# Three in-place ScalarE copies ahead of each scatter product in a two-layer GCN and attention kernel

## The chip, the cores and the metric

The kernel runs on one core of a Trainium2 chip. The metric is device time in microseconds (us) of one execution, as a median over runs.

## What is computed

The reference takes 12,500 nodes with 256 features each and 200,000 edges, sorted by destination. All is float32. Cut to what matters:

```python
h = maximum(layernorm(x), 0)
h = h @ W_pre + b_pre
h = relu(gcn(h, W1, b1));  h = relu(gcn(h, W2, b2))     # each: segment_sum(h[src] * norm, dst)
x = x + (h @ W_post + b_post)
h = maximum(layernorm(x), 0)
xt = (h @ weight).reshape(n, 4, 64)
alpha = softmax(leaky_relu(alpha_l(xt[src]) + alpha_r(xt[dst])), axis=1)
x = x + broadcast(einsum('nh,nhd->nd', alpha[:n], xt[dst[:n]]))
```

The two `gcn` layers gather a row of 256 features for every edge and add it to the edge's destination. That is nearly all of the work.

## The kernel before

**Tiles and chunks.** The edges are cut into chunks of 14 tiles of 128 edges (`J = 14`, 1,792 edges); there are `NCH` = 112 chunks, the last of 9 tiles. Each `gcn` layer is one pass, one call of `convolve`, over all chunks. The destination nodes are cut into `NT` = 98 windows of 128 nodes.

**One tile.** GpSimd (POOL) issues an indirect DMA that gathers 128 rows of the layer's table into a slice of the buffer `fgot` (L1374). TensorE (PE) multiplies it by a one-hot matrix that says which destination within the chunk's window each edge has, and accumulates in PSUM (`facc`, L1382). In float32 that product is two weight loads and two matmuls. The one-hot matrices of a whole chunk, 128 x 14 x 128, are made by a single VectorE (DVE) instruction (`hot_of`, L1241), one chunk ahead, at the third tile of the chunk before; there are three such buffers, `fhot`.

```python
            nc.tensor.matmul(acc, hots[c][:, j, :], got[:, :width], start=(j == 0),
                             stop=(j == nj[c] - 1 and not some))
```

**The first chunks of pass 1.** For the chunks 0 to 3 (`raw`, four buffers) the rows were gathered during the preparation, straight from the input; POOL's gathers in the loop begin with the fifth chunk. In pass 2 `raw` is empty. In pass 1 there are five buffers of a chunk's gathers, in pass 2 four, so POOL can run chunks ahead of PE.

**End of a chunk.** `close` has ScalarE (ACT) copy the sums from PSUM (`fsums`, L1276), and puts two steps into a list of due steps: PE turns the sums 8 tiles later (`fturn`, L1206), DVE adds them 13 tiles later into the window's buffer (`buf`, L1293). When a window is complete, its own steps are listed, counted in tiles from that addition. In pass 1 (`finish1`) they are: 6 tiles later a product on PE (`fpo`, L1417 and L1418); 10 tiles later a Relu on ACT (`fo`, L1422) and its DMA to the second layer's table. In pass 2 (`finish2`): 6 PE `fpz` (L1472); 8 DVE `fy` and ACT `fz` (L1479, L1482); 12 PE `fpo` (L1488); 14 DVE `fx`, `st`, `mv` and ACT `sc`, a square root (L1493 to L1501); 16 DVE, then ACT `h` (L1509); 20 PE `fpt` (L1514); 22 ACT `ht` (L1518); 26 PE `fpx` (L1527); 28 ACT `fxa` (L1535) and two DMAs, issued from ACT's queue (L1536, L1538). Near the end of a pass (`near`, the last three chunks) these steps come one tile after another.

**Order.** Each engine works through its instructions in the order in which the program wrote them: for every tile the gather, the product, and then the steps that are due. Every fifth chunk or so ACT also moves the window buffer's contents (`buf`, L1315, and in pass 1 `sbuf`, L1317).

**After pass 2** comes an attention stage of short gathers (`fal`, L1662) and DVE work.

Of the kernel before, what the change touches and what calls it, by code (L numbers as in the profile page):

```python
# [11 lines left out]
AF = mybir.ActivationFunctionType  # L12
# [401 lines left out]
def fast_path(  # L414
# [26 lines left out]
    nc = tc.nc  # L441
# [6 lines left out]
    NCH = -(-E // CE)  # L448
# [84 lines left out]
    def new_got():  # L533
        return gp.tile([P, J, D1], F32, name="fgot", bufs=RAW + 1)

    raw = [new_got() for c in range(RAW)]
# [616 lines left out]
    def convolve(ep, table, stride, width, ahead, with_sum, psum, prepare, finish, lacking=False,  # L1153
                 raw=(), rows_p=None):
# [12 lines left out]
        def at(t, step, fills=None, then=None):  # L1167
            d = {"t": t, "n": state["n"], "step": step, "fills": fills, "then": then}
            state["n"] += 1
            due.append(d)  # L1170
            return d
# [11 lines left out]
        def run(now=None):  # L1183

            while due:
                d = min(due, key=lambda d: (d["t"], d["n"]))
                if now is not None and d["t"] > now:
                    return
                do(d)
# [49 lines left out]
        def one_hots(h, to):  # L1239
            n = to.shape[1]  # L1240
            nc.vector.tensor_tensor(h, iota_p[:, None, :].to_broadcast([P, n, P]),  # L1241
                                    to[:, :, None].to_broadcast([P, n, P]), ALU.is_equal)

        def hot_of(c):

            n = nj[c]
            h = ep.tile([P, J, P], F32, name="fhot", bufs=3)
            one_hots(h[:, :n, :], to_0 if lacking and c == 0 else to_t[:, c, :n])
            return h

        def new_rows_of():
            if with_sum:
                return new_got()
            return rows_p.tile([P, J, stride], F32, name="fgot", bufs=ahead)

        def late_sums():

            h = ep.tile([P, J, P], F32, name="fhot", bufs=3)
            one_hots(h, to_t[:, 0, :])
            froms = new_rows_of()  # L1260
            assert stride == TW * P
            for i in range(TW):
                one_hots(froms[:, :, i * P:(i + 1) * P], from_0[:, i, :])
            px = psum.tile([P, KC, P], F32, name="fpt", bufs=1)
            for i in range(TW):
                for j in range(J):
                    nc.tensor.matmul(px[:, i, :], froms[:, j, i * P:(i + 1) * P], h[:, j, :],  # L1267
                                     start=(j == 0), stop=(j == J - 1))
            many = work.tile([P, KC, P], F32, name="fz", bufs=2)
            nc.scalar.activation(many, px, AF.Copy)  # L1270
            return many, [load_rows((NT - TW + i) * P, P) for i in range(TW)]

        def close(c, acc, t):
# [64 lines left out]
            at(t + (1 if c + 1 == NCH else 2 if near else 8), turn)  # L1338
            at(t + (2 if c + 1 == NCH else 3 if near else 13), add)

        tiles = [(c, j) for c in range(NCH) for j in range(nj[c])]
        hots = {0: hot_of(0)}
        raw_lohi, raw_m = {}, {}
# [7 lines left out]
        def raw_ahead(c, j):  # L1351

            if j == 1:
                raw_hots(raw_lohi[c])
                raw_m[c] = rows_p.tile([P, CE], F32, name="fsources", bufs=1)
            elif j in (3, 5, 7, 9):
                raw_block(raw_lohi[c], raw_m[c], fpt(), 2 * (j - 3))()
                if j == 9:
                    raw_stats(c)
            elif j + 1 == J:  # L1360
                raw_sum(c, raw_m[c], fpt())()
                raw_scaled(c)

        assert KC == TW
        for t, (c, j) in enumerate(tiles):
            if j == 0:
                acc = psum.tile([P, width], F32, name="facc", bufs=2 if not with_sum else 3)

            if j == 0:
                gots = (raw + [spare])[c] if raw and c <= len(raw) else new_rows_of()  # L1370
            got = gots[:, j, :]
            some = lacking and c == 0
            if c >= len(raw):
                nc.gpsimd.indirect_dma_start(  # L1374
                    out=got, out_offset=None, in_=table[:(NT - TW) * P, :] if some else table[:],
                    in_offset=bass.IndirectOffsetOnAxis(
                        ap=src_0[:, j:j + 1] if some else src_t[:, c, j:j + 1], axis=0))
            if j == 2 and some:
                late = late_sums()
            if j == (5 if some else 2) and c + 1 < NCH:  # L1380
                hots[c + 1] = hot_of(c + 1)
            nc.tensor.matmul(acc, hots[c][:, j, :], got[:, :width], start=(j == 0),  # L1382
                             stop=(j == nj[c] - 1 and not some))
            if some and j == nj[c] - 1:
                for i in range(TW):
                    nc.tensor.matmul(acc, late[0][:, i, :], late[1][i], start=False,
                                     stop=(i == TW - 1))
            if j == nj[c] - 1:
                close(c, acc, t)
            if c + 1 < len(raw):  # L1390
                raw_ahead(c + 1, j)
            run(t)
# [39 lines left out]
    with tc.tile_pool(name="psum1", bufs=1, space=PSUM) as psum, \  # L1432
            tc.tile_pool(name="edges1", bufs=1) as ep, \
            tc.tile_pool(name="fwork1", bufs=2) as work, \
            tc.tile_pool(name="flate1", bufs=1) as late:
        attn = load_late(late)
        convolve(ep, table1, D1, D + 1, 4, True, psum, lambda w: prepare1(work, w),
                 lambda w, b, s, pre, _: finish1(work, psum, w, b, s, pre), raw=raw,
                 rows_p=late)
# [141 lines left out]
    with tc.tile_pool(name="psum2", bufs=1, space=PSUM) as psum, \  # L1581
            tc.tile_pool(name="fwork2", bufs=2) as work, \
            tc.tile_pool(name="edges2", bufs=1) as ep, \
            tc.tile_pool(name="fgots2", bufs=1) as rows_p:
        ep.tile([P, 320], F32, name="apart")
        for c in range(EARLY):
            turn_hots(ap, c, load_ends(work, c, 1), EARLY)
        none = work.tile([P, LW, H], F32, name="none", bufs=1)
        nc.vector.memset(none, 0.0)
        nc.sync.dma_start(table_e[(NT - LW) * P:, :].rearrange("(w p) h -> p w h", p=P), none)  # L1590

        from_all = work.tile([P, CE], I32, name="to_all", bufs=1)
        nc.sync.dma_start(from_all, src[:CE].partition_broadcast(P))
        for i in range(LW):
            nc.vector.tensor_scalar(hot_l[i], from_all, float((NT - LW + i) * P), lane,
                                    op0=ALU.subtract, op1=ALU.is_equal)
        convolve(ep, table2, D, D, 4, False, psum, lambda w: prepare2(work, w),
                 lambda w, b, s, pre, bias: finish2(work, psum, w, b, pre, bias), True,
                 rows_p=rows_p)

        for c in range(1, AC):
            own_rows(c)
# [150 lines left out]
```

## Time and profile before

| | |
|---|---|
| median of 12 runs | 4151.65 us (4146.73 to 4158.75) |
| the profiled execution: time, span | 4160.72 us, 4158.9 us |
| PE matmul busy | 3091.8 us (74%) |
| DVE busy | 1139.5 us (27%) |
| ACT busy | 491.9 us (12%) |
| POOL busy | 3113.8 us (75%) |
| gathers of the two passes (L1374) | 3,056, from 130.6 to 3993.8 us of the span |
| first gather of pass 2 | 2028.50 us |
| granted TensorE clock, mean | 0.797 |

The span is what lies between the first and the last instruction of the profiled execution; its own time is 1.8 us more. Busy shares are averages over the whole span: an engine at 75% can still be the one that everything waits for, if the rest is time that it needs between its instructions. A line of a group gives the busy time, the mean duration of one instruction in ns, then the idle time just before such instructions and what ended it.

### The profile page before, as it was taken

Reading aid. Unit: us, or ns where it says so; the run is one execution under the profiler, and the core shown is the slowest. Engines: PE = TensorE matmul, PEld = TensorE weight load, DVE = VectorE, ACT = ScalarE, POOL = GpSimd, SP = SyncE. Lnnn points to the kernel's source line nnn. Section 1 sums busy time; section 2 is a strip of 40 time slices with the busy share of each in tenths; the row PEclk is TensorE's granted clock in tenths of the full one; section 3 lists DMA queues with packets and bytes.
Section 4 is the critical chain, followed back from the end, with each engine's and each line's share of the span. In section 5 each row is a group of like instructions: output and inputs, shape, how many; then the busy total and the mean of one; then the engine's idle time right before and its main releaser. Section 6 shows DMA issues by size and latency. Waiting matters only on the chain. (4 is left out here: it accounts for less than half of the span.)

```text
span 4158.9 us, 32267 instructions
## 1 busy us (share of the span) xinstructions
PE 3091.8 (74%) x10600; PEld 1979.1 (48%) x10600; DVE 1139.5 (27%) x2421; ACT 491.9 (12%) x1233; POOL 3113.8 (75%) x3299
## 2 busy tenths in 40 slices
PE   6688887877888777877577777777777777777774
PEld 5564444444444444443365554554555545545562
DVE  8532111111111111111232222222222222222238
ACT  5400000000000000000011111111111111111122
POOL 7677777777777777777777777777777777777766
PEclk8697778778777788788688888788878888887876
DMA  9644444444444444444545555555555455555556
GB/s 278 189 126 121 119 119 120 122 120 119 119 122 119 119 119 122 119 118 118 151 123 134 129 128 126 129 130 128 127 128 132 128 127 128 131 125 125 132 163 202
DMA packets 327419, 554.57 MB, mean 133 GB/s; under 512 B 96301, under 2 KB 224836, under 8 KB 327244
## 3 DMA queue, kind: packets, MB, share of 16 engines
q0 software_dynamic: 153520, 414.16, 38.9%
q1 hardware_dynamic: 127878, 121.99, 9.9%
q10 hardware_dynamic: 45846, 16.27, 1.6%
q8 instruction: 87, 1.43, 0.2%
q14 instruction: 88, 0.72, 0.1%
HBM read 498.89 MB, written 53.21 MB: 133 GB/s over the span
## 5 line engine op out<-in xcount | busy, mean ns | idle before, releaser
L1374 POOL DMA_INDIRECT fgot<-ftable,fsrc_t x3056 | 2901.2, 949 | 951.3 <-issue 887.9
L1382 PE MATMUL facc<-fgot,fhot 128*128 128x257 f32 (+1 forms) x6252 | 2326.7, 493 | 902.5 <-DMA fgot<-ftable,fsrc_t 861.8
L1382 PEld LDWEIGHTS facc<-fgot,fhot 128*128 128x128 f32 x6252 | 1260.9, 231 | 1808.7 <-DMA fgot<-ftable,fsrc_t 1361.5
L1293 DVE TENSOR_TENSOR buf<-buf,fturn 128x256 f32 x224 | 94.5, 422 | 1635.9 <-PE fturn L1206 1302.9
L1241 DVE TENSOR_TENSOR fhot<-iota_p,to_t 128x1792 f32<-128x1792 f32 x224 | 448.9, 2004 | 5.4 <-PE fpt L1267 5.3
L1479 DVE SCALAR_TENSOR_TENSOR fy<-rb,fb2c,fpz 128x128 f32<-128x128 f32 x194 | 58.8, 344 | 747.4 <-PE fpz L1472 746.4
L1276 ACT ACTIVATE fsums<-facc 128x257 f32<-128x257 f32 (+1 forms) x224 | 86.1, 384 | 1152.6 <-PE facc L1382 1146.5
L1493 DVE SCALAR_TENSOR_TENSOR fx<-fpo,fdinv,fxb 128x256 f32<-128x256 f32 x97 | 46.9, 484 | 478.7 <-PE fpo L1488 478.7
L1417 PE MATMUL fpo<-wf,buf 128*128 128x256 f32 x388 | 154.4, 542 | 0.4 <-DVE buf L1293 0.4
L1422 ACT ACTIVATE fo<-fpo,fdinv 128x256 f32<-128x256 f32 x97 | 46.0, 474 | 749.7 <-PE fpo L1418 749.7
L1417 PEld LDWEIGHTS fpo<-wf,buf 128*128 128x128 f32 x388 | 111.9, 289 | 28.3 <-DVE buf L1293 0.7
L1472 PE MATMUL fpz<-buf,fwb 128*128 128x128 f32 x776 | 123.7, 312 | 0.0
L1472 PEld LDWEIGHTS fpz<-buf,fwb 128*128 128x128 f32 x776 | 120.9, 234 | 2.5 <-DVE fy L1479 0.3
L1488 PE MATMUL fpo<-fwo,fz 128*128 128x256 f32 x388 | 118.1, 432 | 0.1
L1206 PE MATMUL fturn<-fident,self 128*128 128x128 f32 x396 | 84.6, 299 | 37.7 <-DMA to_all<-in_src_dram 24.6
L1662 POOL DMA_INDIRECT fal<-table_l,fsrc_t x84 | 81.7, 973 | 25.6 <-issue 22.9
L1206 PE MATMUL fturn<-fident,fsums 128*128 128x128 f32 x448 | 95.5, 299 | 0.5 <-ACT fsums L1276 0.5
L1652 PE MATMUL fends<-rows,hot_t 128*128 128x260 f32 x168 | 67.5, 567 | 33.7 <-ACT fxg L1654 33.2
L1518 ACT ACTIVATE ht<-fpt 128x256 f32<-128x256 f32 x97 | 37.2, 384 | 466.2 <-PE fpt L1514 466.2
L668 POOL DMA_INDIRECT fgot<-in_x_dram,raw_i x56 | 73.6, 1315 | 15.4 <-issue 15.4
L1206 PEld LDWEIGHTS fturn<-fident,fsums 128*128 128x128 f32 x448 | 70.1, 157 | 31.1 <-issue 8.0
L1418 PE MATMUL fpo<-bb,fins 2*128 2x256 f32 x194 | 84.3, 520 | 0.0
(267 smaller groups left out, 1729.9 us busy)
## 6 DMA issues: line engine op xcount, KB each, us to landing
fgot<-ftable,fsrc_t POOLq DMA_INDIRECT x3056
self<-ftable SPq DMA_DIRECT2D x99, 128.0 KB
self<-ftable SPq DMA_DIRECT2D x97, 130.0 KB
ftable<-fo ACTq DMA_DIRECT2D x98, 128.0 KB
kept_x<-fx SPq DMA_DIRECT2D x98, 128.0 KB
fxb<-in_x_dram SPq DMA_DIRECT2D x97, 128.0 KB
fxr<-kept_x SPq DMA_DIRECT2D x13, 896.0 KB
out_dram<-fres SPq DMA_DIRECT2D x13, 896.0 KB
```

What stands on the lines that cost most here:

```text
L668: nc.gpsimd.indirect_dma_start(out=raw[c][:, j, :D], out_offset=None, in_=x[:], in_offset=bass.IndirectOffsetOnAxis(ap=raw_i[:, k:k + 1], ...
L1206: nc.tensor.transpose(v["pt"][:, i * KC + k, :], rows[:, k * P:(k + 1) * P], ident)
L1241: nc.vector.tensor_tensor(h, iota_p[:, None, :].to_broadcast([P, n, P]), to[:, :, None].to_broadcast([P, n, P]), ALU.is_equal)
L1276: nc.scalar.activation(sb, acc, AF.Copy)
L1293: nc.vector.tensor_add(b, b, v["pt"][:, :KC, :])
L1374: nc.gpsimd.indirect_dma_start(out=got, out_offset=None, in_=table[:(NT - TW) * P, :] if some else table[:], in_offset=bass.IndirectOffset ...
L1382: nc.tensor.matmul(acc, hots[c][:, j, :], got[:, :width], start=(j == 0), stop=(j == nj[c] - 1 and not some))
L1417: nc.tensor.matmul(po, buf[:, k, :P], wf[:, k, :], start=(k == 0), stop=False)
L1418: nc.tensor.matmul(po, fs, bb, start=False, stop=True)
L1472: nc.tensor.matmul(pz[:, m, :], wb[:, k, m * P:(m + 1) * P], buf[:, k, :P], start=(k == 0), stop=(k == KC - 1))
L1488: nc.tensor.matmul(po, v["z"][:, m, :], wo[:, m, :], start=(m == 0), stop=(m == KC - 1))
L1662: nc.gpsimd.indirect_dma_start(out=al[:, i, :], out_offset=None, in_=(table_l if c else table_e)[:], in_offset=bass.IndirectOffsetOnAxis(a ...
```

## The change

Ahead of each product with gathered rows, ScalarE copies the tile's one-hot columns (128 x 128, float32) onto themselves, three times. The values stay the same. This is done for every chunk from number `len(raw)` to the last but one: in pass 1 that is from the fifth chunk on, in pass 2, where `raw` is empty, from the first.

```diff
+        def spread(h):
+            for _ in range(3):
+                nc.scalar.activation(h, h, AF.Copy)
+
         tiles = [(c, j) for c in range(NCH) for j in range(nj[c])]
...
             if j == (5 if some else 2) and c + 1 < NCH:
                 hots[c + 1] = hot_of(c + 1)
+            if len(raw) <= c < NCH - 1:
+                spread(hots[c][:, j, :])
             nc.tensor.matmul(acc, hots[c][:, j, :], got[:, :width], start=(j == 0),
                              stop=(j == nj[c] - 1 and not some))
```

That is 107 chunks in pass 1 and 111 in pass 2, with 14 tiles of three copies each: 9,156 instructions on ACT. The instructions of the other engines and their order stay as they were. In the changed program the second and third copy of a tile wait for ACT's own copy before, each product waits for ACT beside its gather, and each making of one-hots by DVE waits for ACT too.

## The prediction

> **What bounds the kernel now.** I read the page's costliest groups first, for the engine whose idle time nobody else explains. The columns are: busy us, mean ns of one | idle us before it, and what ended it.
>
> ```profile
> L1374 POOL DMA_INDIRECT fgot<-ftable,fsrc_t x3056 | 2901.2, 949 | 951.3 <-issue 887.9
> L1382 PE MATMUL facc<-fgot,fhot 128*128 128x257 f32 (+1 forms) x6252 | 2326.7, 493 | 902.5 <-DMA fgot<-ftable,fsrc_t 861.8
> ```
>
> PE's idle time ends with a gather's landing. POOL's idle time ends with "issue", that is, nothing that the profile shows. The two POOL numbers make 3852.5 us for 3056 gathers, and gathers lie from 130.6 to 3993.8 us: POOL issues them with hardly a break, and that is the kernel's length. Next I read the waits, for POOL's waits on others.
>
> ```profile
> POOL fgot L1374 <- issue: 891.9, 2899, 7.9
> POOL fgot L1374 <- PE facc L1382: 39.3, 104, 7.1
> ```
>
> Only 39.3 us stand against PE, and of the 104 nearly all are the usual 0.30 us; the one of 7.1 is at 147 us, in the raw chunks, which the change leaves alone. Then the timeline of a chunk in the middle of pass 2 (start, us, engine), from the 11th tile on, which the later sums use.
>
> ```profile
> 3016.18 0.94 POOL L1374 DMA_INDIRECT fgot<-ftable,fsrc_t  x1 [0.30 <-issue]
> 3016.51 0.70 PE L1382 MATMUL facc<-fgot,fhot 128*128 128x256 f32 x2 [0.22 <-DMA fgot<-ftable,fsrc_t]
> 3017.43 0.95 POOL L1374 DMA_INDIRECT fgot<-ftable,fsrc_t  x1 [0.30 <-issue]
> 3017.59 0.17 ACT L1535 ACTIVATE fxa<-fpx 128x4 f32<-128x4 f32 x1 [2.80 <-PE fpx L1527]
> 3017.79 0.33 ACTq L1536 DMA_DIRECT2D table_l<-fxa  x1
> 3018.16 1.02 ACTq L1538 DMA_DIRECT2D table_e<-fxa  x1
> 3018.56 0.48 DVE L1493 SCALAR_TENSOR_TENSOR fx<-fpo,fdinv,fxb 128x256 f32<-128x256 f32 x1 [3.89 <-PE fpo L1488]
> 3019.75 0.29 ACT L1501 ACTIVATE sc<-mv,feps 128x1 f32<-128x1 f32 x1 [1.99 <-DVE mv L1499]
> ```
>
> POOL's starts are 1.253 us apart, whatever ACT and DVE do meanwhile; 14 of them make a chunk of 17.54 us. So the question is whether ACT and PE together still get through a chunk in 17.54 us. If they do, up to four chunks of buffers hide every delay within a chunk.
>
> **The price of a copy.** No 128 x 128 copy from SBUF to SBUF is in the trace. The nearest rows, by shape on ACT:
>
> ```profile
> L1482 ACT ACTIVATE fz<-fy 128x256 f32<-128x256 f32 x98 | 40.9, 417 | 219.7 <-DVE fy L1479 219.7
> L1315 ACT ACTIVATE buf<-buf 128x640 f32<-128x640 f32 x46 | 33.9, 737 | 99.1 <-DVE buf L1293 89.8 <-DMA ftable<-fo 6.7 <-ACT fxa L1535 1.8
> L1317 ACT ACTIVATE sbuf<-sbuf 1x320 f32<-1x320 f32 x24 | 10.9, 453 | 3.0 <-DVE sbuf L1296 3.0
> ```
>
> From 417 to 737 ns for 384 elements is 0.833 ns each, so 128 elements cost 417 - 107 = 310 ns by the first row and 453 - 160 = 293 by the third. I take 0.30. For the wait of one copy on the copy before, ACT's timeline in the preparation has such a pair, and a run of instructions without it:
>
> ```profile
> 92.61 3.53 ACT L990 ACTIVATE fgot<-fgot,fnb,fsc 128x256 f32<-128x256 f32 x7
> 96.24 0.16 ACT L941 ACTIVATE fdeg<-fdegs 128x21 f32<-128x21 f32 x1
> 96.44 0.22 ACT L942 ACTIVATE froot<-fdeg 128x21 f32<-128x21 f32 x1
> ```
>
> The dependent one starts 0.20 after one of 0.16: a gap of 0.04, in other pairs 0.03. The seven independent ones of 584 ns start 0.49 apart: they overlap by 0.09. A tile's copies then take 3 x 0.30 + 2 x 0.03 - 0.09 = 0.87 us, a chunk's 14 x 0.87 = 12.2 us.
>
> **ACT's chunk in pass 1.** To the 12.2 come fsums 0.38, fo 0.47 - 0.09, its DMA issue 0.35, and buf and sbuf in 23 of 111 chunks, (0.74 + 0.45) x 23 / 111 = 0.25: 13.6. And one new wait: fsums needs the last tile's product, which now needs the last tile's copies; behind fsums in ACT's queue are the next chunk's copies, and for those PE waits. After the copies comes a product of 0.70 us (the row above, at the full clock), hand-overs of 0.05 and 0.04, and the overlap of 0.09 is lost: 0.88. At half clock a product took 1.22 (3022.99 us), so 1.4. Together 14.4 to 15.0, at least 2.5 us under POOL's chunk: hidden.
>
> **ACT's chunk in pass 2.** 12.2, and with one window's steps fsums 0.38, h 0.59 - 0.09, ht 0.38 - 0.09, fz 0.42 - 0.09, fxa and its two DMA issues 1.0 (median second issue 0.44), less 0.05, sc 0.29 and buf 0.74 x 23 / 111: 2.9, together 15.1. Two waits come on top. At fsums 0.88 again. At sc: ACT gets there after the copies of two tiles and fxa, 1.74 + 0.95 = 2.7 us from the end of the 11th tile's copies; mv is ready after 0.05, that tile's product 0.70, and the 2.54 us from its end at 3017.21 to sc at 3019.75, that is 3.3: a wait of 0.6. The sum is 16.6. A chunk in which no window ends costs 12.2 + 0.3 + 0.88 = 13.4. With 98 windows in 112 chunks the mean is 16.2 us, 1.3 under POOL's.
>
> That is at PE's full clock. In half-microsecond slices the granted clock falls to 0.50 at 3005.2 us, after PE idled from 3002.1, and is back at 1.00 at 3012.2, after 5.5 us of work. At half clock throughout the wait at fsums is 1.4, and at sc the product takes 0.52 and fpx and fpo (1.35 us) another 1.35 more, a wait of 2.5: 19.0 with a window, 18.4 in the mean, 0.9 us over POOL's chunk. From 2600 to 3300 us the clock was 0.82, which is 36% of the time at 0.50; by that share I take 16.2 + 0.36 x 2.2 = 17.0 us, 0.5 under. So pass 2 is hidden too, but narrowly.
>
> The Trainium skill, "TensorE: Matmul & The Clock Gate", section "HAM oscillation", warns of idle gaps over about 3.4 us, after which the array falls back to half clock. The new gaps (fsums and one tile's copies, some 1.3 us) stay under that and by the rule would keep the clock up, so that the sum would be 16.2 rather than 17.0. The same page calls ACT's queue strict FIFO, which speaks against the change, since each of the two waits holds up the copies behind it; the sum above has both.
>
> **What else moves.** Gathers, products and steps keep their order on POOL, PE, DVE and SP. DVE's making of one-hots now waits for copies two chunks old: nothing. ACT's DMA issues stand behind up to 14 tiles' copies, but a tile's step follows that tile's copies, and 12.2 us of 17.54 leaves ACT in time. At the start of pass 2, 12 tiles wait behind the late sums at 2087 us; before, PE took them in 5.35 us, now 12 x 0.87 = 10.4; POOL next needs that buffer at 2105. At the ends there is no slack for free. Pass 2 began when the last rows of the table had landed, 0.98 us after a gather instead of 0.30, so a late ACT in chunk 110 passes through: 0 to 0.9 us. In pass 2's last chunk but one the steps come a tile apart, and each tile could take 0.87 + 0.88 instead of 1.25: 7 us late over 14 tiles, of which PE's waits in the last chunk (2.48 and 1.40) give 3.9 back: 0 to 3.1. I take 2 us of these 0 to 4. None of it can fall below nothing, as the chain only gets a new member.
>
> The profiled execution has 4160.72 us for a span of 4158.9, and is 9.1 us (0.2%) above the median of 4151.65; I add differences to the median: 4151.65 + 2 = 4153.7.
>
> **Rivals.** (1) ACT becomes the bound of pass 2. Its waits for PE outgrow the margin, the buffers fill after some chunks, and POOL starts to wait on PE. It decides from a mean chunk of 17.54 us on, that is from 12 ns more per copy at the mixed clock (31 at the full one). For it: ACT's queue in order, PE's half clock. Against it: a late PE works without breaks, and in 2087 to 2110 us, where it was behind, it took 24 matmuls in 5.35 us, full clock. Price at half clock throughout: 0.86 x 111 = 95 us, 4247; halfway 4200. (2) PE gains. With fewer long idle times its clock stays up, and the chain after the last gather, where matmuls took 2.05, 1.91, 1.37, 1.01 and 0.99 us, would take half of that: 3.7 us less, 4148, still within 0.2%. More would need POOL's 1.253 us to shrink, and nothing in the rows moves it. (3) The copies cost nothing because they are not there: no, the changed program holds 9,156 of them, each with its waits.
>
> **How the numbers follow.** 0.2%, or 8.3 us, is about what a measurement of this kernel can tell from no change. Hidden, with 0 to 4 us at the ends and rival (2) within the bound: 0.60. Rival (1): 0.34, from a few us to 4247 and, if copies are dearer, beyond. Faster by more than 8.3 us: 0.06, for something that I don't see. The likeliest case gives 4153.7 and by itself holds 4146 to 4160. The range goes up to rival (1)'s price, 4247, and down to the lowest run, 4146.
>
> **What would show it.** Right: POOL's starts stay 1.253 us apart in both passes, with waits on PE still near 40 us; ACT busy near 491.9 + 9156 x 0.30 = 3240 us; PE's waits move in part from gathers to copies; copies of 0.29 to 0.31 us, 0.33 apart. Wrong: POOL waiting on PE in hundreds of us in pass 2, a chunk of more than 17.54 us there, or copies over 0.32 us.

## The result, and the profile after

| | before | after |
|---|---|---|
| median | 4151.81 us (28 runs, 4146.73 to 4158.91) | 4194.53 us (7 runs, 4187.79 to 4194.99) |
| the profiled execution: time, span | 4160.72, 4158.9 us | 4193.94, 4192.1 us |
| granted TensorE clock, mean | 0.797 | 0.839 |

The changed kernel takes 1.0098 times as long, 95% interval 1.0088 to 1.0107: 42.7 us more. Ten of the twelve runs told further down were made on four chips on which the kernel before itself took 4,920 to 4,938 us in place of 4,152, so that they are given as ratios to it. The costliest groups of the page after, in the columns of before:

```profile
L1378 POOL DMA_INDIRECT fgot<-ftable,fsrc_t x3056 | 2892.6, 947 | 946.7 <-issue 899.1
L1388 PE MATMUL facc<-fgot,fhot 128*128 128x257 f32 (+1 forms) x6252 | 2302.6, 486 | 1035.1 <-ACT fhot L1343 774.6
L1343 ACT ACTIVATE fhot<-fhot 128x128 f32<-128x128 f32 x9156 | 2562.7, 304 | 281.5 <-ACT fo L1428 38.7
```

POOL's gathers cost what they did, and it still sits idle between them only for "issue". What ended PE's waits has changed from gathers to copies. A copy takes 304 ns. In the view of waits (us in total, times, longest) PE's waits for copies come first, and POOL has one long wait that was 12.9 us before:

```profile
PE facc L1388 <- ACT fhot L1343: 774.6, 1041, 2.8
POOL fal L1668 <- DMA table_l<-fxl: 53.9, 1, 53.9
POOL fgot L1378 <- PE facc L1388: 27.3, 72, 5.7
```

POOL hardly waits for PE within the passes (27.3 us, less than before's 39.3; the one of 5.7 is at 157 us, in pass 1's first chunks). It waits once at length, for 53.9 us, at the start of the attention stage, for the last rows of `table_l`, which the last window of pass 2 writes. The same place in the timelines, first of before, then of after:

```profile
4015.16 0.95 POOL L1662 DMA_INDIRECT fal<-table_e,fsrc_t  x1 [12.89 <-DMA table_l<-fxl]
```

```profile
4047.24 0.95 POOL L1668 DMA_INDIRECT fal<-table_e,fsrc_t  x1 [53.88 <-DMA table_l<-fxl]
```

The wait is 41.0 us longer; the instruction starts 32.1 us later, as POOL's last gather starts 8.9 us earlier (3984.91 for 3993.8). That fits with the two profiled executions, which differ by only 33.2 us: in the profiled execution of before each gather took 949 ns for 947, which is 8.6 us of busy time over 3056 gathers, and that execution stood 9.1 us above its median.

The chunk in the middle of pass 2, from the view that the prediction read:

```profile
3014.74 0.95 POOL L1378 DMA_INDIRECT fgot<-ftable,fsrc_t  x1 [0.30 <-issue]
3015.99 0.94 POOL L1378 DMA_INDIRECT fgot<-ftable,fsrc_t  x1 [0.30 <-issue]
3016.32 0.29 ACT L1507 ACTIVATE sc<-mv,feps 128x1 f32<-128x1 f32 x1 [1.09 <-DVE mv L1505]
3016.52 0.97 ACT L1343 ACTIVATE fhot<-fhot 128x128 f32<-128x128 f32 x3
3017.55 0.70 PE L1388 MATMUL facc<-fgot,fhot 128*128 128x256 f32 x2 [1.56 <-ACT fhot L1343]
3018.28 0.38 ACT L1276 ACTIVATE fsums<-facc 128x256 f32<-128x256 f32 x1 [0.79 <-PE facc L1388]
```

POOL's starts are 1.25 us apart, whatever ACT does. ACT stands 1.09 us at `sc`, PE then stands 1.56 us for the copies behind it, and ACT stands 0.79 us at `fsums` for that product: each waits for the other in turn.

**Where the time lies.** For every chunk of pass 2, the distance from the start of its last gather (POOL) to the start of `fsums` (ACT) says how far PE and ACT are behind POOL. Read from the timelines, in us:

| chunk | before | after | more |
|---|---|---|---|
| 0 | 48.6 | 54.6 | 6.0 |
| 1 | 35.4 | 48.8 | 13.4 |
| 2 | 23.8 | 43.9 | 20.1 |
| 3 | 10.4 | 39.9 | 29.5 |
| 4 | 3.6 | 38.5 | 34.9 |
| 5 | 3.5 | 36.9 | 33.4 |
| 15 | 5.1 | 44.0 | 38.9 |
| 20 | 5.1 | 43.0 | 37.9 |
| 60 | 5.5 | 47.4 | 41.9 |
| 108 | 6.2 | 46.2 | 40.0 |
| 109 | 3.6 | 44.6 | 41.0 |
| 110 | 3.6 | 51.5 | 47.9 |
| 111 | 6.7 | 48.9 | 42.2 |

Both kernels start pass 2 some 50 us behind, because POOL gathers on while the late sums are made (what the first chunk of pass 2 needs of the last windows, whose rows are not yet in the table when its gathers begin). Before, PE works that off in four chunks; after, the distance stops falling at 37 us and creeps up to 46. In the last chunk it is 42.2 us more than before, where the medians differ by 42.7. Of these, 33.4 are there by chunk 5, another 6.6 come from chunk 5 to 108 (after 9.3, before 2.7), and the last three chunks add 2.2.

The part from chunk 5 to 108 is no even drift: 7.1 of after's 9.3 us are there by chunk 15, where `fsums` moves on by 18.2 us a chunk; from chunk 15 to 108 it moves on by 17.54 us, and the distance grows by only 2.2 us in 93 chunks. The first nine windows have more work on ACT than the later ones, 0.66 us each: `fxa` has 264 columns in place of 4 (0.39 us for 0.17), and a third DMA follows it (0.44 us). The last steps of eight of them fall in these ten chunks, which makes 5.3 us; that fits the 7.1, but no run shows it by itself.

```profile
2222.64 0.39 ACT L1541 ACTIVATE fxa<-fpx 128x264 f32<-128x264 f32 x1
2223.06 0.33 ACTq L1542 DMA_DIRECT2D table_l<-fxa  x1
2223.42 0.45 ACTq L1544 DMA_DIRECT2D table_e<-fxa  x1
2223.91 0.44 ACTq L1546 DMA_DIRECT2D table_r<-fxa  x1
```

The first chunks on ACT, and the same stretch of before on PE:

```profile
2095.99 0.38 ACT L1276 ACTIVATE fsums<-facc 128x256 f32<-128x256 f32 x1 [1.65 <-PE facc L1392]
2096.27 12.45 ACT L1343 ACTIVATE fhot<-fhot 128x128 f32<-128x128 f32 x42
2109.51 0.38 ACT L1276 ACTIVATE fsums<-facc 128x256 f32<-128x256 f32 x1 [0.79 <-PE facc L1388]
```

```profile
2096.91 6.21 PE L1382 MATMUL facc<-fgot,fhot 128*128 128x256 f32 x28
```

A chunk whose rows have all landed costs 13.52 us from `fsums` to `fsums` after, 42 copies and one wait; before, PE needed 6.21 us for its 28 matmuls. From then on ACT's chunk is the measure: from chunk 5 to chunk 108 `fsums` moves on by 17.60 us a chunk, POOL's gathers by 17.51.

### The profile page after: what moved, and what is told of

Read it like the earlier page. It is cut to its first block, busy times and chain, and to the rows that moved or that the text cites. A ratio compares the mean times of both kernels' runs of the same rounds, so it can differ in the third digit from the quotient of the medians.

```text
span 4192.1 us, 43997 instructions
## 1 busy us (share of the span) xinstructions
PE 2995.3 (71%) x10600; PEld 1840.0 (44%) x10600; DVE 1139.9 (27%) x2421; ACT 2970.9 (71%) x10389; POOL 3106.5 (74%) x3299
## 5 line engine op out<-in xcount | busy, mean ns | idle before, releaser
L1388 PE MATMUL facc<-fgot,fhot 128*128 128x257 f32 (+1 forms) x6252 | 2302.6, 486 | 1035.1 <-ACT fhot L1343 774.6
L1343 ACT ACTIVATE fhot<-fhot 128x128 f32<-128x128 f32 x9156 | 2562.7, 304 | 281.5 <-ACT fo L1428 38.7
L1388 PEld LDWEIGHTS facc<-fgot,fhot 128*128 128x128 f32 x6252 | 1171.1, 225 | 2012.0 <-ACT fhot L1343 1746.6
L1507 ACT ACTIVATE sc<-mv,feps 128x1 f32<-128x1 f32 x98 | 28.8, 294 | 139.5 <-DVE mv L1505 137.1
L1423 PE MATMUL fpo<-wf,buf 128*128 128x256 f32 x388 | 119.6, 438 | 0.3 <-DVE buf L1293 0.3
L1488 ACT ACTIVATE fz<-fy 128x256 f32<-128x256 f32 x98 | 40.8, 416 | 105.3 <-DVE fy L1485 105.3
L1206 PE MATMUL fturn<-fident,self 128*128 128x128 f32 x396 | 80.8, 288 | 37.1 <-DMA to_all<-in_src_dram 24.3
L1494 PE MATMUL fpo<-fwo,fz 128*128 128x256 f32 x388 | 105.8, 395 | 0.3 <-ACT fz L1488 0.3
L1423 PEld LDWEIGHTS fpo<-wf,buf 128*128 128x128 f32 x388 | 91.2, 235 | 20.0 <-DVE buf L1293 0.8
```

The source lines that it names most:

```text
L1206: nc.tensor.transpose(v["pt"][:, i * KC + k, :], rows[:, k * P:(k + 1) * P], ident)
L1343: nc.scalar.activation(h, h, AF.Copy)
L1423: nc.tensor.matmul(po, buf[:, k, :P], wf[:, k, :], start=(k == 0), stop=False)
L1494: nc.tensor.matmul(po, v["z"][:, m, :], wo[:, m, :], start=(m == 0), stop=(m == KC - 1))
```

## The experiments

**Theories.** S, the start of pass 2: ACT's chunk is as long as POOL's, so what is lost while the backlog stands is never worked off and comes out at the end. D, the drift: every chunk of pass 2 is somewhat too long, and the loss is even over its 111 chunks. A third was that the copies themselves load something, so that only their number counts. Chunks are counted from zero, and each ratio is to the kernel before on the same chip.

**Copies in pass 1 only, copies in pass 2 only.**

```diff
-            if len(raw) <= c < NCH - 1:
+            if with_sum and len(raw) <= c < NCH - 1:      # pass 1 only
+            if not with_sum and c < NCH - 1:              # pass 2 only
```

> The copies in pass 1 only, 4,494 of them. Both theories say that the loss comes from pass 2: 4152 us, at most 4156, with POOL's starts 1.25 us apart and pass 2 beginning within 2 us of where it began before. The other reading, that the copies cost by their number wherever they are, expects half of the 42.7 us, 4172.

> The copies in pass 1 only, as e1, which was measured while the kernel before itself took 4938 us. Where that takes 4152 us: both theories expect 4152, at most 4156; half of the 42.7 us, 4172, if the copies cost by their number wherever they are.

> The copies in pass 2 only, 4,662 of them. Both theories expect the whole loss, 4190 to 4196 us. By number alone it would be 4174.

Measured: pass 1 only 1.0228 (1.0200 to 1.0255) and on a second chip 1.0221 (1.0167 to 1.0276); pass 2 only 1.0805 (1.0780 to 1.0830). Most of the cost is pass 2's there too. But pass 1 is not free there, as it was in the profile of after, so these runs do not show where the 42.7 us lie, and S and D are not told apart by them.

**Copies in pass 2 from its chunk 5 on** (all of pass 1's kept; the chunks 0 to 4 have none, which is five chunks and not four, as two of the expectations further down have it).

```diff
-            if len(raw) <= c < NCH - 1:
+            if (len(raw) if with_sum else 5) <= c < NCH - 1:
```

> As the change, but in pass 2 the copies begin with chunk 5 instead of 0 (8,946 copies, 2% fewer). Theory S (start of the pass): ScalarE's chunk takes as long as POOL's, so that PE can never work off the 31 us which it falls behind in chunks 0 to 4; without copies there it has caught up by chunk 5, and only some 7 us of drift and some 7 us at the end of the pass are left: 4160 to 4168 us. Theory D (drift): every chunk of pass 2 is a little too long, 42.7 us over 111 chunks; five chunks fewer take 2 us off: 4192.

> As e3: the change, but in pass 2 the copies begin with chunk 5. Where the kernel before takes 4152 us, theory S (PE never works off the 31 us that it falls behind at the start of pass 2) expects 4160 to 4168 us; theory D (each chunk of pass 2 a little too long) expects 4192.

> Three copies as in the changed kernel, but pass 2's copies begin only with its fifth chunk, so that the four chunks left over from the late sums are worked off at TensorE's own pace. In a session in which the kernel before takes about 4,152 us: by the start of pass 2 (S) the delay of about 31 us is never built up; the gathers and products of pass 2 then run as close together as before, POOL's last wait on table_l is 15 to 25 us in place of 53.9, and the time is 4,160 to 4,172 us. By the drift (D) every chunk of pass 2 gives its part of the loss, four chunks in 112 change nothing that can be measured, and it is 4,188 to 4,195 us. In a session in which TensorE is itself the bound, as in the two before, about 9% over the kernel before, and it decides nothing.

Measured: 1.1034 (1.1008 to 1.1060), 1.0940 (1.0884 to 1.0996) and 1.0925 (1.0852 to 1.0998). The reason that it decides nothing here is in the timeline of the first of these runs:

```profile
3516.42 0.51 PE L1533 MATMUL fpx<-fwg,ht 128*128 128x4 f32 x4
3516.78 1.11 PE L1494 MATMUL fpo<-fwo,fz 128*128 128x256 f32 x4
3522.82 0.17 ACT L1541 ACTIVATE fxa<-fpx 128x4 f32<-128x4 f32 x1 [5.23 <-remote]
3522.88 0.48 DVE L1499 SCALAR_TENSOR_TENSOR fx<-fpo,fdinv,fxb 128x256 f32<-128x256 f32 x1 [10.70 <-remote]
```

`fpx` has its modelled end at 3516.93, and its reader starts at 3522.82; "remote" is a release that the profile ties to no instruction. This chunk of pass 2 took 24.1 us, and POOL waited 916 us for PE in all. Here the readers start 5 to 6 us after PE's modelled end, ACT's queue stands behind the reader, and pass 2 is bound by the hand-over between PE and ACT, not by POOL. What delays the results there is not in the profile and stays open.

**Neither the first five nor the last three chunks of pass 2.**

```diff
-            if len(raw) <= c < NCH - 1:
+            if (len(raw) if with_sum else 5) <= c < NCH - (1 if with_sum else 3):
```

> Three copies, but in pass 2 only for the chunks 5 to 108: neither the four chunks left over from the late sums nor the last three have any. That leaves out 196 tiles of copies less than 98, that is 7 of pass 2's 111 chunks; the 104 in the middle and all of pass 1 keep theirs. In a session in which the kernel before takes about 4,152 us: by the start of pass 2 (S), what the copies cost lies in these few chunks, so that the time falls to 4,152 to 4,162 us. By the drift (D) the 104 chunks in the middle carry the loss, and it stays at 4,185 to 4,195 us. In a session in which the kernel before takes over 4,900 us, with TensorE as the bound, it is some 9% over it and decides nothing.

Measured: 1.0977 (1.0952 to 1.1003), within the three values above. Here the chunks in the middle carry the loss (24.3 us a chunk from chunk 5 to 108), and leaving out the ends of pass 2 changes nothing that can be measured.

**Two copies for three.**

```diff
-            for _ in range(3):
+            for _ in range(2):
```

> Two copies of a tile instead of three. ScalarE's chunk in pass 2 falls from 17.6 us by 14 x 0.34 = 4.8 to some 12.8 us, so PE works off its 31 us within 7 chunks. Theory S: 4152 to 4157 us, no loss beyond the ends. By number alone two thirds of the loss would stay, 4180 us.

Measured: 1.0678 (1.0623 to 1.0732). With a third fewer copies most of the cost is left. Where PE and ACT are the bound this decides nothing between S and D either.

**The same copies, 11 tiles ahead of their product** (in pass 2 from its third chunk on; the copies of the two chunks before that stand at their product).

```diff
+            if j >= 3 and first <= c + 1 < NCH - 1:
+                spread(hots[c + 1][:, j - 3, :])
+            if j < 3 and first <= c < NCH - 1:
+                spread(hots[c][:, j + 11, :])
```

> All 9,156 copies, but each tile's copies stand 11 tiles ahead of its product in ScalarE's queue (in pass 2 from chunk 2 on; chunks 0 and 1 as in the change). If ScalarE's chunk in pass 2 is 14.5 us of work and 3.1 us of waits for PE and VectorE that in turn waited for the copies, the waits mostly go, the chunk is 14.5 to 15.5 us, and PE catches up within about 15 chunks: 4152 to 4160 us. If it is the copies' sheer load, on ScalarE or on the memory, 4185 to 4195 as with the change.

> As e6: all 9,156 copies, each 11 tiles ahead of its product (in pass 2 from chunk 2 on). Where the kernel before takes 4152 us: 4152 to 4160 us if the waits between ScalarE and PE make the loss, 4185 to 4195 if the load itself does.

Measured: 1.0253 (1.0226 to 1.0279) and 1.0157 (1.0103 to 1.0212), beside 1.1034 and 1.0940 on the same chips for copies right ahead of the product. The number of copies is nearly the same (the runs from chunk 5 have 8,946, these 9,156). How far `fsums` moves on per chunk of pass 2, from chunk 5 to 108, shows it directly; the two values are those of two chips:

| copies in pass 2 | us a chunk |
|---|---|
| none (pass 1 only) | 20.9, 20.9 |
| three, 11 tiles ahead | 21.3, 20.9 |
| two, at the product (second chip only) | 23.6 |
| three, at the product, from chunk 5 | 24.3, 24.1 |

So on these chips the third theory falls: placed ahead, all the copies add 0.4 us a chunk on one chip and nothing on the other; at the product they add over 3 us, of which a third fewer copies takes off only 0.5. What costs there is that a product stands behind copies that stand, in ACT's queue, behind a reader of PE. Whether copies placed ahead would also save the 42.7 us of the result was not run.

**TensorE relieved, copies from chunk 0 or from chunk 5 of pass 2.** Beside these two the kernel before took 4157.35 us. Of a chunk's 14 products the 12 inner ones take 32 columns, so those sums are left out; in pass 2 the eighth tile has a fourth copy (about 0.3 us a chunk).

```diff
+                if j == 7 and not with_sum:
+                    nc.scalar.activation(hots[c][:, j, :], hots[c][:, j, :], AF.Copy)
-            nc.tensor.matmul(acc, hots[c][:, j, :], got[:, :width], start=(j == 0),
+            few = width if j == 0 or j == nj[c] - 1 else 32
+            nc.tensor.matmul(acc[:, :few], hots[c][:, j, :], got[:, :few], start=(j == 0),
                             stop=(j == nj[c] - 1 and not some))
```

> The changed kernel with TensorE relieved, so that POOL may set the pace even where TensorE is slow: of a chunk's 14 products the 12 inner ones take 32 of the 256 (257) columns, which leaves those sums out of the output. In pass 2 the eighth tile of each chunk gets a fourth copy, to make up on ACT for the shorter waits. If POOL sets the pace, the two passes end when its gathers do, about 3,985 us, and the rest takes what it took. By the start of pass 2 (S): 4,175 to 4,200 us, POOL waits 40 to 60 us for the last rows of table_l, and the distance between a chunk's last gather and its sums grows by 20 to 30 us over the first five chunks of pass 2. By the drift (D): that distance is small in the first chunks and grows evenly to the last. If TensorE is still the bound, the time is over 4,300 us with POOL's waits on TensorE in hundreds of us, and nothing is decided.

> The same relieved kernel, but in pass 2 copies (the fourth at the eighth tile too) only from the fifth of its chunks counted from zero on, so that the backlog of the late sums is worked off at TensorE's pace. By the start of pass 2 (S) it is 20 to 35 us faster than the relieved kernel with copies from the first chunk. By the drift (D) it is 0 to 4 us faster. If TensorE is still the bound, the two differ by what the session makes of them, and nothing is decided.

Measured: 4445.2 us, ratio 1.0695 (1.0677 to 1.0713), from chunk 0; 4406.83 us, 1.0601 (1.0583 to 1.0619), from chunk 5. The times are neither theory's: over 4,300 us, with POOL's waits for PE in hundreds of us, they are the case that by the expectation decides nothing. The aim was missed in an unforeseen way: with the narrow products the granted clock stayed at half. The windows of after, then of the relieved kernel, in columns of PE, PEld, DVE, ACT and POOL busy, then the clock:

```profile
2160.00:4000.00 1840.00, 1307.04 (x5006) 854.09 (x5005) 484.31 (x1036) 1407.56 (x4995) 1386.79 (x1467) 0.87 0.51 129
```

```profile
2160.00:4000.00 1840.00, 1279.57 (x4421) 1029.16 (x4422) 427.74 (x914) 1271.66 (x4511) 1234.02 (x1306) 0.51 0.45 115
```

So this pair comes close to the price case of the prediction's rival (1), pass 2 at half clock throughout, though with narrow products and a fourth copy. Its distances behind POOL, as in the table above:

| chunk | copies from chunk 0 | from chunk 5 |
|---|---|---|
| 0 | 56.6 | 45.4 |
| 4 | 45.5 | 4.1 |
| 10 | 66.1 | 24.8 |
| 20 | 61.0 | 47.8 |
| 60 | 60.8 | 60.8 |
| 108 | 62.8 | 61.7 |
| 111 | 61.2 | 60.9 |

At this clock a drift is real: `fsums` moves on by 19.88 us a chunk, with copies from chunk 5 the distance grows as soon as they begin, at some 61 to 66 us the buffers are full, and from then on POOL waits for PE, 286.1 and 249.9 us in all. And the first chunks come on top: the two kernels differ by 38.4 us, 20 to 35 expected by S and 0 to 4 by D. The five chunks in which ACT replaces a PE that was catching up cost about what they cost in the changed kernel (33.4 us by chunk 5). But the hand-over between ACT and PE is the bound of both of these kernels, so that whatever the first chunks take is added; that such a delay also lasts where ACT and POOL are level, as in the changed kernel, rests on the table of distances, not on this pair.

**What follows for the changed kernel.** By its table of distances 33 of the 42 us are there by chunk 5 and never worked off, which is S; some 7 come after, most of them in the first ten chunks, and 2 in the last three. D, an even loss in every chunk, does not fit that. This is read from the two profiled executions; no run shows it by itself. Open is the direct run, full products with copies from chunk 5, where the kernel before takes 4,152 us: the three runs of it were made on chips where that takes over 4,900. The runs point to no version that beats both kernels.

## Why the prediction was right and where it was wrong

The time, 4194.53 us, lies in the range, in the part that rival (1) opened. The likeliest case, hidden, with 4153.7 us, was not what happened, and most of the loss came from a place that the prediction priced at nothing, the start of pass 2. That it lies within the range is luck in so far: the upper bound stood for a pass 2 at half clock throughout, which the changed kernel did not have.

**What held.** The price of a copy: 304 ns for 0.30 us, 0.88 us a tile for 0.87, 13.52 us for a chunk without a window for 13.4. Pass 1 is hidden: pass 2's first gather starts at 2025.11 us for 2028.50, and in the relieved kernel, at a clock of 0.50 in pass 1, at 2027.91. POOL's pitch did not move. The last chunk but one, with its steps one tile apart, took 24.4 us, 7 late as worked out, and by the end of the last all but 1.2 us of that had come back (41.0 to 42.2 in the table), within the 0 to 3.1. ACT's busy time is 2970.9 us for 3240, as the page counts overlapping copies once, which the sum did not do.

**The step that failed: ACT's chunk in pass 2.** It was priced at 17.0 us, 0.5 under POOL's, with two waits, at `fsums` and at `sc`. The trace has three large ones. ACT's waits between 2160 and 4000 us, 104.5 chunks of after, then 92.6 of the relieved kernel:

```profile
ACT sc L1507 <- DVE mv L1505: 129.8, 91, 1.7
ACT fz L1488 <- DVE fy L1485: 95.6, 92, 2.0
ACT fsums L1276 <- PE facc L1388: 84.3, 104, 1.3
```

```profile
ACT sc L1510 <- DVE mv L1508: 199.9, 75, 2.8
ACT fsums L1276 <- PE facc L1391: 120.5, 93, 1.3
ACT fz L1491 <- DVE fy L1488: 117.4, 81, 1.5
```

Per chunk that is 1.24 us at `sc`, 0.81 at `fsums` and 0.91 at `fz` after, at a clock of 0.87; 2.16, 1.30 and 1.27 at 0.51. `sc` was priced 0.6 at the full clock and 2.5 at half, `fsums` 0.88 and 1.4: both near. `fz`, which waits for DVE's `fy` and that for PE's `fpz`, was counted as work alone, 0.33 us. With the measured clock the prediction's own sum is 16.2 + 26% of 2.2 = 16.8 us; with `fz` 17.7; measured 17.60 from chunk 5 to 108, and 17.54 from chunk 15. At half clock it is 18.4 + 0.3 for the fourth copy = 18.7; with `fz` 20.0; measured 19.88, with narrower products than the sum has. By this sum one wait of 0.9 us left out decided the sign: the margin was 0.5, or 0.7 with the measured clock. The third DMA of the first nine windows and their wider `fxa`, 0.66 us each, were left out too; neither the prediction nor the part ahead of it names them.

**What the margin was needed for.** "At the start of pass 2, 12 tiles wait" priced one chunk, 10.4 us for 5.35, and asked only when POOL next needs that buffer. Nearly three more chunks had been gathered by then, each 13.5 us on ACT for 6.3 on PE; by chunk 5, 33 us were lost. That up to "four chunks of buffers hide every delay within a chunk" held for POOL, which hardly waited; but buffers only put a delay off. With the forecast slack of 0.5 us a chunk, 33 us would have been gone after some 66 chunks; with a slack of 17.51 - 17.60 = -0.09 they stayed, and the attention stage, which needs the last window, waited for them.

**The rivals.** (1) had the right engine, and of its signs a chunk of more than 17.54 us came (17.60). But POOL waiting on PE in hundreds of us did not (27.3 us after); that appears only in the relieved kernel at half clock (286.1 us). Its price for that, 4247, was low: measured 4445.2 with the fourth copy, that is 288 us more than before for 95; `fz` at 1.27 us in 111 chunks, the fourth copy at 0.3 and the first chunks at 38 us make 212 for the missing 193. (2) came half true: the clock rose from 0.797 to 0.839, and from the last `fsums` to POOL's `fal` it took 13.4 us for 14.6, 1.2 us of its 3.7.

**The clock.** The rule of the Trainium skill that the prediction weighed ("TensorE: Matmul & The Clock Gate", section "HAM oscillation") points the right way for the changed kernel: PE's longest idle time between 2200 and 3900 us is 2.84 us after, for 4.41 before with ten over 3.4, and the clock is 0.87 for 0.82. It is not 1.00, though, with no idle time over 3.4 us left, and in the relieved kernel none there is over 3.33 us while the clock is 0.51. Short gaps alone did not keep it up.

## What to carry to other kernels

Work that is "hidden" under a pacing engine must be compared with that engine's chunk together with every wait that it meets in its own in-order queue, one line for each reader of another engine; here two of three were counted, and the third was larger than the margin. Buffers don't remove a delay, they carry it: ask where the kernel starts behind (here pass 2, after the late sums), at what rate it catches up, and who needs the last result. The distance from a producer to its consumer, chunk by chunk, shows in one table whether a loss comes from the start, from a drift or from the end; take enough chunks, as what looked like a drift here was mostly ten chunks with more work.

## What was not expected of the hardware

Less work for TensorE made the kernel slower: 4445.2 us for 4194.53, of which the fourth copy, 0.3 us in each of 111 chunks, is some 33. With 12 of 14 products cut to 32 columns the clock fell from 0.87 to 0.51 in pass 2, so that a 32-column product of the relieved kernel still took 390 ns in the mean, where the 256-column product of the changed kernel took 479, and the products that stayed whole took 710:

```profile
L1391 PE MATMUL facc<-fgot,fhot 128*128 128x32 f32 x5356 | 1482.4, 390 | 566.1 <-ACT fhot L1343 270.6 <-ACT fhot L1389 172.7 <-DMA fgot<-ftable,fsrc_t 117.0
L1391 PE MATMUL facc<-fgot,fhot 128*128 128x256 f32 x448 | 271.7, 710 | 368.5 <-ACT fhot L1343 362.7 <-DMA fgot<-ftable,fsrc_t 4.1 <-DVE sc L1513 1.8
```
